# Expert layers: an expert's first unit is queued behind the next unit's transposes

## The chip, the core and the metric

The kernel runs on one core of one Trainium2 chip. That core has five engines that each take their own instructions in order: TensorE (PE in the profile; its weight loads, PEld, overlap its matmuls), VectorE (DVE), ScalarE (ACT), GpSimd (POOL) and SyncE (SP), which here only starts transfers. The metric is device microseconds of one execution, as the median of several timed runs. Besides the timed runs there is one execution taken by the hardware profiler, with a start and a duration for every instruction; "the span" is the time from its first to its last instruction. "The granted clock" is the share of full speed at which TensorE was allowed to run.

## The reference

The kernel computes four residual blocks on 8192 tokens of 256 features. Each block adds a normalised output to the running activations:

```
x = x + layernorm(attention_with_memory(layernorm(x)))
x = x + layernorm(mixture_of_experts_0(layernorm(x)))
x = x + layernorm(linear_attention(layernorm(x)))
x = x + layernorm(mixture_of_experts_1(layernorm(x)))
```

Only the two mixtures of experts matter here. Each has 8 experts. A gate sends every token to one expert; the tokens of an expert are ranked, and those beyond its capacity (512 in the first mixture, 1024 in the second) are dropped. An expert is two products with a nonlinearity between them:

```
h  = act(tokens_of_expert @ w1[e])      # 256 -> 1024, gelu in the first, relu in the second
eo = h @ w2[e]                          # 1024 -> 256
out = x + gate * eo[slot of the token]
```

All arithmetic is in float32. The output is (8, 1024, 256).

## The kernel before

The kernel goes through four stages: the attention with memory and its update (up to about 1292 us of the profiled span, the routing of the first mixture included), the first mixture's experts (about 1292 to 1602 us), the linear attention with the second routing (to about 2084 us), and the second mixture's experts (to the end, 2557.8 us). Both mixtures run through one function, `experts` (L954), called at L660 and L810. The routing has left, in DRAM, a row for every token and, on chip, the list of token numbers of every expert's slots and the number of tokens of every expert.

`experts` cuts each expert's slots into units of 256 slots (`UT`). The first mixture has two units per expert, 16 in all; the second has four, 32 in all. For a unit, these helpers do the work:

- `fetch(u)` (L974): two indirect transfers started by GpSimd (L814) gather 2 x 128 token rows into tile `d`. Five such tiles exist.
- `enter(d)` (L981): normalisation. VectorE takes the statistics (L144, L145: tiles `st_d`, `mv_d`, `ve_d`), GpSimd raises them to the power -1/2 (L133, tile `r_d`), VectorE writes the normalised rows `xh` with two instructions (`ln_apply`, L159) and scales `sc_d`.
- `turn(xh)` (L1004): four transposes on TensorE (L1009) into a PSUM tile `tp`, which VectorE copies to `dT` (one copy, L1011, in the second mixture; two instructions with scale and shift, L1014, in the first). Three `dT` and three `xh` tiles exist.
- `load(e)` (L1018): the two weight matrices `wa` and `wb` of an expert, started by SyncE, two sets of tiles.
- `products(u, ...)` (L1029): the unit's matmuls. The first product (L1037, tile `h`) is 16 matmuls in the code and 32 records in the profile, since a float32 matmul is two of them; ScalarE applies the nonlinearity (L1041 or L1045, `hT`); the second product (L1051, tile `op`) is 32 records. Then `finish0` (L635) or `finish1` (L786) add the residual and normalise on VectorE (L640 or L790 is its first instruction, per 128 rows), with a power on GpSimd (L133, `rs`), and the store goes out through SyncE (L658) or as a GpSimd scatter (L806).

The loop at L1064 goes over the units in order. In turn `u` it first starts the loads of the next expert, then `fetch(u+3)`, `enter(u+2)` and `turn(u+1)`, and then `products(u)`. An expert's first unit (`q == 0`) always runs and is not in a branch. Its later units stand in `tc.If(n[e] > q * UT)` (L1073): they are skipped on the chip where the expert has too few tokens. In the profiled execution 14 of 16 units ran in the first mixture and 20 of 32 in the second (1088 records of L1037, 32 for each unit).

The order of the instructions on each engine is not that of the code. A planner at build time lays them out: it follows the code's order as priority, but lets an instruction that it believes ready go ahead of an earlier one on the same engine that it believes is still waiting. A branch is one block for it: nothing from outside is mixed into it, though whole helpers can be put ahead of it or behind it. So parts of a first unit's `products`, which are outside any branch, may be placed among the `enter` and `turn` instructions of later units. On the chip each engine then follows its list strictly. `tc.issue_after(ins)` is the means to tell the planner more: every instruction that is traced inside it on the engine of `ins` must come behind `ins` in that engine's list. It adds no wait for `ins` to finish and no instruction.

Of the kernel before, what the change touches and what calls it, by code (L numbers as in the profile page):

```python
# [13 lines left out]
ALU = mybir.AluOpType  # L14
# [4 lines left out]
B, S, H = 8, 1024, 256  # L19
NTOK = B * S  # L20
P = 128
# [6 lines left out]
UT = TU * P  # L28
# [33 lines left out]
def sandwich_kernel(ctx: ExitStack, tc: tile.TileContext, a, out: bass.AP):  # L62
# [594 lines left out]
    def store0(s0, o):  # L657
        nc.sync.dma_start(_rows(slot0_d[s0 : s0 + UT, :]), o)  # L658

    experts(env, tok0_d, idx0[0], idx0[2], CAP0, a["wi"], a["wo"], AF.Gelu, None, None, finish0, store0, gbc)  # L660


# [150 lines left out]
def gather(nc, dst, src, idx):  # L813
    nc.gpsimd.indirect_dma_start(out=dst, out_offset=None, in_=src,  # L814
                                 in_offset=bass.IndirectOffsetOnAxis(ap=idx, axis=0),
                                 bounds_check=src.shape[0] - 1, oob_is_err=False)


class Router:
# [83 lines left out]
    def finish(self, pool):  # L903

        nc, nb = self.env.nc, self.nb
        tf = self.sb.tile([P, nb], F32, tag="tf", name="tf")
        nc.vector.tensor_scalar(tf, self.tab, -1.0, 0.0, ALU.add, ALU.max)
        got = pool.tile([P, nb], I32, name=f"got{nb}")
        nc.vector.tensor_copy(got, tf)
        tp = self.sb.tile([P, nb], F32, tag="tp", name="tp")  # L910
        nc.vector.tensor_scalar(tp, self.tab, 0.0, float(FAR), ALU.is_equal, ALU.mult)
        nc.vector.scalar_tensor_tensor(tp, self.tab, -1.0, tp, ALU.add, ALU.add)
        put = pool.tile([P, nb], I32, name=f"put{nb}")
        nc.vector.tensor_copy(put, tp)

        pc = self.ps.tile([P, NE], F32, tag="rt", name="pc")
        nc.tensor.matmul(pc, self.env.ones, self.before[:, :, TG], start=True, stop=True)
        cnt = pool.tile([P, NE], I32, name=f"cnt{nb}")
        nc.vector.tensor_copy(cnt, pc)
        return got, put, cnt  # L920
# [33 lines left out]
def experts(env, src, idx, cnt, cap, w1, w2, act, b1, b2, finish, store, gb):  # L954


    tc, nc, small = env.tc, env.nc, env.small
    with ExitStack() as ph:
        p2 = ph.enter_context(tc.tile_pool(name="e2", bufs=2))
        pc = ph.enter_context(tc.tile_pool(name="ec", bufs=1))  # L960
        p3 = ph.enter_context(tc.tile_pool(name="e3", bufs=3))
        p5 = ph.enter_context(tc.tile_pool(name="e5", bufs=5))
        pf = ph.enter_context(tc.tile_pool(name="ef", bufs=FC // 2 + 2))
        pst = ph.enter_context(tc.tile_pool(name="est", bufs=2, space=PSUM))
        psh = ph.enter_context(tc.tile_pool(name="esh", bufs=3, space=PSUM))
        pso = ph.enter_context(tc.tile_pool(name="eso", bufs=3, space=PSUM))
        if b1 is not None:
            b1c = pc.tile([P, NE * FC], F32, name="b1c")
            nc.sync.dma_start(b1c, b1)
        nq = cap // UT  # L970
        units = [(e, q) for e in range(NE) for q in range(nq)]
        nu = len(units)

        def fetch(u):  # L974
            d = p5.tile([P, TU, H + 1], F32, tag="d", name="d")
            for j in range(TU):
                i = u * TU + j
                gather(nc, d[:, j, :], src, idx[:, i : i + 1])
            return d

        def enter(d):  # L981

            mv = env.stats(env.tiles(d), "d")
            ve = small.tile([P, 2, TU], F32, tag="ve_d", name="ve_d")
            r = small.tile([P, 2, TU], F32, tag="r_d", name="r_d")
            nc.vector.tensor_scalar(ve[:, 0, :], mv[:, :, 1], EPS, None, ALU.add)
            if gb is None:
                env.rsqrt(r[:, 0, :], ve[:, 0, :], TU)
                rs = r[:, 0, :]
            else:  # L990
                nc.vector.tensor_scalar(ve[:, 1, :], mv[:, :, 1], 1.0 + EPS, EPS * EPS, ALU.mult, ALU.add)
                env.rsqrt(r.rearrange("p a t -> p (a t)"), ve.rearrange("p a t -> p (a t)"), 2 * TU)
                rs = r[:, 1, :]
            sc = p5.tile([P, 2, TU], F32, tag="sc_d", name="sc_d")
            s = d[:, :, H]
            if gb is not None:
                nc.vector.tensor_tensor(sc[:, 0, :], s, r[:, 0, :], ALU.mult)
            nc.vector.scalar_tensor_tensor(sc[:, 1, :], s, EPS, s, ALU.mult, ALU.mult)
            xh = p3.tile([P, TU, H], F32, tag="xh", name="xh")
            for j in range(TU):  # L1000
                env.ln_apply(xh[:, j, :], d[:, j, :H], mv, rs, j)
            return xh, sc

        def turn(xh):  # L1004
            dT = p3.tile([P, HC, UT], F32, tag="dT", name="dT")
            t = pst.tile([P, HC, UT], F32, tag="tp", name="tp")
            for c in range(HC):
                for j in range(TU):
                    nc.tensor.transpose(t[:, c, j * P : (j + 1) * P], xh[:, j, c * P : (c + 1) * P], env.ident)  # L1009
            if gb is None:  # L1010
                nc.vector.tensor_copy(dT, t)  # L1011
            else:
                for c in range(HC):
                    nc.vector.tensor_scalar(dT[:, c, :], t[:, c, :], gb[:, 0, c : c + 1], gb[:, 1, c : c + 1],  # L1014
                                            ALU.mult, ALU.add)
            return dT

        def load(e):  # L1018
            wa = p2.tile([P, HC, FF], F32, tag="wa", name="wa")
            nc.sync.dma_start(wa, w1[e].rearrange("(k p) f -> p k f", p=P))  # L1020
            wb = p2.tile([P, FC, H], F32, tag="wb", name="wb")
            nc.sync.dma_start(wb, w2[e].rearrange("(k p) f -> p k f", p=P))
            b2r = None
            if b2 is not None:
                b2r = p2.tile([P, H], F32, tag="b2r", name="b2r")
                nc.sync.dma_start(b2r, b2[e].partition_broadcast(P))
            return wa, wb, b2r

        def products(u, d, dT, sc, w):  # L1029
            e = units[u][0]  # L1030
            wa, wb, b2r = w
            hT = []
            for f0 in range(0, FC, 2):
                t = psh.tile([P, 2, UT], F32, tag="h", name="h")
                for f in range(2):
                    for c in range(HC):
                        nc.tensor.matmul(t[:, f, :], wa[:, c, (f0 + f) * P : (f0 + f + 1) * P], dT[:, c, :],  # L1037
                                         start=(c == 0), stop=(c == HC - 1))
                h = pf.tile([P, 2, UT], F32, tag="hT", name="hT")
                if b1 is None:  # L1040
                    nc.scalar.activation(h, t, act)  # L1041
                else:
                    for f in range(2):
                        i = e * FC + f0 + f
                        nc.scalar.activation(h[:, f, :], t[:, f, :], act, bias=b1c[:, i : i + 1])  # L1045
                hT.append(h)

            def po(j):
                t = pso.tile([P, H], F32, tag="o", name="op")
                for f in range(FC):  # L1050
                    nc.tensor.matmul(t, hT[f // 2][:, f % 2, j * P : (j + 1) * P], wb[:, f, :], start=(f == 0),  # L1051
                                     stop=(f == FC - 1))
                return t

            store(u * UT, finish(p2, d, po, b2r, sc))

        w = {0: load(0)}
        n = [nc.values_load(cnt[0:1, e : e + 1], min_val=0, max_val=NTOK,
                            skip_runtime_bounds_check_because="the experts' counts add up to NTOK")
             for e in range(NE)]  # L1060
        d = {u: fetch(u) for u in range(3)}
        x = {u: enter(d[u]) for u in range(2)}
        dT = {0: turn(x[0][0])}
        for u, (e, q) in enumerate(units):  # L1064
            if q == 0 and e + 1 < NE:
                w[e + 1] = load(e + 1)
            if u + 3 < nu:
                d[u + 3] = fetch(u + 3)
            if u + 2 < nu:
                x[u + 2] = enter(d[u + 2])  # L1070
            if u + 1 < nu:
                dT[u + 1] = turn(x[u + 1][0])
            with (tc.If(n[e] > q * UT) if q else nullcontext()):  # L1073
                products(u, d[u], dT[u], x[u][1], w[e])


# [41 lines left out]
```

## Time and profile before

| | |
|---|---|
| median of three timed runs | 2580.8 us (2579.83 to 2585.32) |
| the profiled execution's own time | 2559.46 us |
| its span | 2557.8 us |
| mean granted TensorE clock | 0.908 |
| TensorE busy | 2084.5 us, 81% |
| VectorE, ScalarE, GpSimd busy | 1156.3, 681.7, 749.7 us |
| first mixture's experts, 1292 to 1602 us | TensorE busy 227.32 of 310.00 us, granted clock 0.85 |
| second mixture's experts, 2084 to 2557.8 us | TensorE busy 314.88 of 473.80 us, granted clock 0.82 |

The profiled execution is 21.3 us shorter than the median of the timed runs, and a difference worked out in the trace is therefore added to the median, not compared with it. A row of the timeline has a start, a duration, the engine, the code line, the operation, the tile written and the tiles read, the shapes, how many instructions of the kind follow one another ("x32"), and in brackets the idle time of the engine before it with what ended that idle time. Consecutive rows of one engine show that engine's order, as the planner laid it out. A row of the windows gives the window, its length, the busy time of the engine with its number of instructions, the granted clock, and the transfers' share and rate.

### The profile page before, as it was taken

To read this page: it belongs to the slowest core of one execution; us is meant where nothing else is said; L and a number is where in the kernel's file an instruction comes from. 1 tells how busy PE (TensorE), PEld (TensorE's weight loads), DVE (VectorE), ACT (ScalarE), POOL (GpSimd) and SP (SyncE) were. 2 spreads that over 40 slices of the span, in tenths; PEclk is the share of its full clock that TensorE was granted. 3 is DMA by queue.
4 is the path that set the end of the run, shared out by engine and by line. 5 is a ranking of instruction groups with operands and counts; after the bars stand their busy time and mean duration, and the time that the engine had idled before them with its cause. 6 is when DMAs were issued, how large, how long until landed. Compare 5 with 4: busy or idle time off the path is not lost. (4 is left out here: it accounts for less than half of the span.)

```text
span 2557.8 us, 25355 instructions
## 1 busy us (share of the span) xinstructions
PE 2084.5 (81%) x8441; PEld 1442.0 (56%) x8441; DVE 1156.3 (45%) x4272; ACT 681.7 (27%) x1187; POOL 749.7 (29%) x811
## 2 busy tenths in 40 slices
PE   5999999998999899889758778689898846885387
PEld 4556555555565556556547566346555545664276
DVE  4445453356455645564533333046565643333232
ACT  3554554232323232322101111223332201111021
POOL 2121220134343433343441221741111123333322
PEclk8999999899999999999869889799999958887698
DMA  4110100201010001000051320111111141122300
GB/s 137 45 50 34 50 25 32 96 25 33 25 40 27 34 25 41 25 25 17 17 157 54 95 91 9 52 33 42 42 42 42 50 116 61 60 68 70 94 23 16
DMA packets 89010, 129.31 MB, mean 51 GB/s; under 512 B 8403, under 2 KB 74104, under 8 KB 88740
## 3 DMA queue, kind: packets, MB, share of 16 engines
q1 hardware_dynamic: 74612, 98.23, 11.6%
q0 software_dynamic: 10640, 24.32, 3.7%
q10 hardware_dynamic: 3616, 4.99, 0.6%
q8 instruction: 74, 1.21, 0.2%
q14 instruction: 68, 0.56, 0.1%
HBM read 86.99 MB, written 46.82 MB: 52 GB/s over the span
## 5 line engine op out<-in xcount | busy, mean ns | idle before, releaser
L1037 PE MATMUL h<-dT,wa 128*128 128x256 f32 x1088 | 271.4, 411 | 4.1 <-issue 2.4
L182 PE MATMUL mm<-x2T,w_W1T 128*128 128x512 f32 x512 | 249.9, 630 | 0.0
L1037 PEld LDWEIGHTS h<-dT,wa 128*128 128x128 f32 x1088 | 225.3, 210 | 43.4 <-issue 7.9
L1051 PE MATMUL op<-wb,hT 128*128 128x256 f32 x1088 | 240.4, 379 | 0.0
L550 PE MATMUL ff<-w_W2T,fT 128*128 128x256 f32 x1024 | 231.1, 381 | 0.0
L1051 PEld LDWEIGHTS op<-wb,hT 128*128 128x128 f32 x1088 | 206.7, 190 | 28.1
L1009 PE MATMUL tp<-ident,xh 128*128 128x128 f32 x192 | 39.8, 359 | 219.8 <-DVE xh L159 219.8
L550 PEld LDWEIGHTS ff<-w_W2T,fT 128*128 128x128 f32 x1024 | 191.1, 190 | 24.5 <-issue 0.5
L1045 ACT ACTIVATE hT<-h,b1c 128x256 f32<-128x256 f32 x160 | 67.1, 470 | 399.0 <-PE h L1037 399.0
L1009 PEld LDWEIGHTS tp<-ident,xh 128*128 128x128 f32 x192 | 28.5, 174 | 230.8 <-issue 140.9
L182 PEld LDWEIGHTS mm<-x2T,w_W1T 128*128 128x128 f32 x512 | 98.9, 204 | 98.8 <-issue 98.1
L545 ACT ACTIVATE fT<-mm,cols 128x512 f32<-128x512 f32 x128 | 88.0, 687 | 199.8 <-PE mm L182 199.7
L594 POOL TENSOR_TENSOR e<-euler,d 128x32 f32<-128x32 f32 x16 | 87.0, 5439 | 179.8 <-DVE d L845 179.8
L702 PE MATMUL kv<-w_WqkvT,xnT 128*128 128x512 f32 x256 | 123.0, 614 | 5.0 <-ACT xnT L690 4.9
L814 POOL DMA_INDIRECT d<-tok_d,got x96 | 100.0, 1042 | 75.3 <-DMA wb<-in_w_dram 16.5
L695 PE MATMUL pm<-kv 128*128 128x257 f32 x256 | 73.2, 411 | 44.2 <-ACT kv L707 38.0
L133 POOL TENSOR_TENSOR rs<-ve,mhalf 128x2 f32<-128x2 f32 x34 | 24.0, 707 | 289.4 <-DVE ve L644 191.6
L695 PEld LDWEIGHTS pm<-kv 128*128 128x128 f32 x256 | 46.8, 197 | 92.7 <-issue 66.3
L1041 ACT ACTIVATE hT<-h 128x512 f32<-128x512 f32 x56 | 33.3, 597 | 239.7 <-PE h L1037 239.7
L507 ACT ACTIVATE moT<-mm,bmo 128x512 f32<-128x512 f32 x32 | 22.0, 687 | 263.0 <-PE mm L182 263.0
L790 DVE TENSOR_TENSOR o<-op,b2r 128x256 f32<-128x256 f32 x40 | 16.9, 423 | 151.7 <-PE op L1051 150.6
L843 DVE TENSOR_REDUCE mx<-lg 128x4 f32<-128x32 f32 x32 | 6.1, 191 | 173.8 <-PE lg L840 173.8
(308 smaller groups left out, 4067.5 us busy)
## 6 DMA issues: line engine op xcount, KB each, us to landing
tok_d<-xa SPq DMA_DIRECT2D x16, 514.0 KB, 3.4
tok_d<-xf SPq DMA_DIRECT2D x16, 514.0 KB, 3.5
xg<-in_x_dram SPq DMA_DIRECT2D x16, 512.0 KB, 3.9
x1T_d<-x1T SPq DMA_DIRECT2D x16, 512.0 KB, 3.3
x1T<-x1T_d SPq DMA_DIRECT2D x16, 512.0 KB, 3.3
xa<-in_x_dram SPq DMA_DIRECT2D x16, 512.0 KB, 3.9
wa<-in_wi_dram SPq DMA_DIRECT2D x8, 1024.0 KB, 6.6
wb<-in_wo_dram SPq DMA_DIRECT2D x8, 1024.0 KB, 9.1
```

The lines of the kernel that those rows point to most:

```text
L182: mm = nc.tensor.matmul(t, w[:, k, o * P : (o + 1) * P], v, start=(k == 0), stop=(k == len(k_in) - 1))
L545: lambda o, t: nc.scalar.activation(fT[o], t, AF.Silu, bias=col("b1", o)))
L550: mm = nc.tensor.matmul(t, fT[f][:, j * P : (j + 1) * P], w2_[:, f, :], start=(f == 0), stop=(f == FC - 1))
L594: nc.gpsimd.tensor_tensor(e, env.euler, d, ALU.pow)
L695: mm = nc.tensor.matmul(pm[d], kvs[j][:, d * P : (d + 1) * P], kvs[j][:, H:], start=(first and j == 0), stop=(last and j == TG - 1))
L702: nc.tensor.matmul(t, xnT[:, c, j * P : (j + 1) * P], wqkv[:, c, H:], start=(c == 0), stop=(c == HC - 1))
L814: nc.gpsimd.indirect_dma_start(out=dst, out_offset=None, in_=src, in_offset=bass.IndirectOffsetOnAxis(ap=idx, axis=0), bounds_check=src.sh ...
L1009: nc.tensor.transpose(t[:, c, j * P : (j + 1) * P], xh[:, j, c * P : (c + 1) * P], env.ident)
L1037: nc.tensor.matmul(t[:, f, :], wa[:, c, (f0 + f) * P : (f0 + f + 1) * P], dT[:, c, :], start=(c == 0), stop=(c == HC - 1))
L1041: nc.scalar.activation(h, t, act)
L1045: nc.scalar.activation(h[:, f, :], t[:, f, :], act, bias=b1c[:, i : i + 1])
L1051: nc.tensor.matmul(t, hT[f // 2][:, f % 2, j * P : (j + 1) * P], wb[:, f, :], start=(f == 0), stop=(f == FC - 1))
```

## The change

`enter` and `turn` now also return instructions: `enter` the last `xh` instruction, `turn` the last transpose and the last copy to `dT`. In the loop, the products of a first unit are traced inside `tc.issue_after` for three instructions: the last `xh` instruction of unit `u+2` (VectorE), the last transpose of unit `u+1` (TensorE) and the last copy to `dT` of unit `u+1` (VectorE). So every TensorE instruction of these products comes behind that transpose in TensorE's list, and every VectorE instruction of them behind the other two in VectorE's. The instructions of the products on ScalarE, GpSimd and SyncE get no such order. Units in branches are as they were. No instruction is added or taken away.

```
-                env.ln_apply(xh[:, j, :], d[:, j, :H], mv, rs, j)
-            return xh, sc
+                last = env.ln_apply(xh[:, j, :], d[:, j, :H], mv, rs, j)
+            return xh, sc, last
...
-                    nc.tensor.transpose(t[:, c, j * P : (j + 1) * P], xh[:, j, c * P : (c + 1) * P], env.ident)
+                    tr = nc.tensor.transpose(t[:, c, j * P : (j + 1) * P], xh[:, j, c * P : (c + 1) * P], env.ident)
             if gb is None:
-                nc.vector.tensor_copy(dT, t)
+                ev = nc.vector.tensor_copy(dT, t)
             else:
                 for c in range(HC):
...
+                    ev = nc.vector.tensor_scalar(dT[:, c, :], t[:, c, :], gb[:, 0, c : c + 1], gb[:, 1, c : c + 1],
+                                                 ALU.mult, ALU.add)
-            return dT
+            return dT, tr, ev
...
-        dT = {0: turn(x[0][0])}
+        dT = {0: turn(x[0][0])[0]}
         for u, (e, q) in enumerate(units):
...
             if u + 2 < nu:
                 x[u + 2] = enter(d[u + 2])
+            first = []
+            if u + 2 < nu:
+                first.append(x[u + 2][2])
             if u + 1 < nu:
-                dT[u + 1] = turn(x[u + 1][0])
-            with (tc.If(n[e] > q * UT) if q else nullcontext()):
+                dT[u + 1], *did = turn(x[u + 1][0])
+                first += did
+            with ExitStack() as order:
+                if q:
+                    order.enter_context(tc.If(n[e] > q * UT))
+                else:
+                    for ins in first:
+                        order.enter_context(tc.issue_after(ins.ins))
                 products(u, d[u], dT[u], x[u][1], w[e])
```

## The prediction

> **What bounds the kernel now.** I read the page first, then the table of waits for the two expert stages, then TensorE's timeline through both, then VectorE's and GpSimd's around a few first units, and last the granted clock. The page's costliest groups and the waits of the two stages (engine, line, releaser, total, times, longest):
>
> ```profile
> L1009 PE MATMUL tp<-ident,xh 128*128 128x128 f32 x192 | 39.8, 359 | 219.8 <-DVE xh L159 219.8
> ...
> PE tp L1009 <- DVE xh L159: 71.4, 9, 9.7
> ...
> PE tp L1009 <- DVE xh L159: 148.4, 9, 25.1
> ```
>
> In both stages TensorE's idle time is one kind of wait: the transposes of a unit wait for its normalised rows. 71.4 of the 219.8 us lie in the first mixture, 148.4 in the second. Its other gaps there come to a few us, so the stage's length is TensorE's work plus these waits. TensorE's order in the first mixture, around expert 2, and the start of expert 1 in the second:
>
> ```profile
> 1353.04 7.07 PE L1037 MATMUL h<-dT,wa 128*128 128x256 f32 x32
> 1359.95 7.07 PE L1051 MATMUL op<-wb,hT 128*128 128x256 f32 x32
> 1366.86 1.03 PE L1037 MATMUL h<-dT,wa 128*128 128x256 f32 x4
> 1377.08 1.22 PE L1009 MATMUL tp<-ident,xh 128*128 128x128 f32 x4 [9.19 <-DVE xh L159]
> 1378.09 8.58 PE L1037 MATMUL h<-dT,wa 128*128 128x256 f32 x28
> 1386.51 7.07 PE L1051 MATMUL op<-wb,hT 128*128 128x256 f32 x32
> 1393.42 0.60 PE L1009 MATMUL tp<-ident,xh 128*128 128x128 f32 x4
> ...
> 2140.76 1.99 PE L1009 MATMUL tp<-ident,xh 128*128 128x128 f32 x8 [21.11 <-DVE xh L159]
> 2143.09 9.31 PE L1037 MATMUL h<-dT,wa 128*128 128x256 f32 x32 [0.34 <-issue]
> ```
>
> Unit 4 is expert 2's first. Four of its 32 h-matmuls stand ahead of unit 5's transposes and fill 0.9 us of the wait; 28 stand behind. In the second mixture all 32 stand behind. What the transposes of unit 5 wait for is a chain through GpSimd and VectorE:
>
> ```profile
> 1372.32 1.09 POOL L814 DMA_INDIRECT d<-tok_d,got  x1 [0.25 <-DVE mv_d L145]
> 1373.44 0.74 POOL L133 TENSOR_TENSOR o<-ve,mhalf 128x2 f32<-128x2 f32 x1
> 1374.36 1.06 POOL L814 DMA_INDIRECT d<-tok_d,got  x1 [0.18 <-issue]
> 1375.45 1.05 POOL L133 TENSOR_TENSOR r_d<-ve_d,mhalf 128x4 f32<-128x4 f32 x1
> ...
> 1371.87 0.16 DVE L991 TENSOR_SCALAR ve_d<-mv_d 128x2 f32<-128x2 f32 x1
> ...
> 1376.61 0.73 DVE L159 TENSOR_SCALAR xh<-d,mv_d,r_d 128x256 f32<-128x256 f32 x2
> ...
> 1379.62 0.99 DVE L1014 TENSOR_SCALAR dT<-tp,gbc 128x256 f32<-128x256 f32 x2
> 1390.17 0.48 DVE L640 SCALAR_TENSOR_TENSOR o<-d,sc_d,op 128x256 f32<-128x256 f32 x1 [9.55 <-PE op L1051]
> ```
>
> Nothing in it reads what the four matmuls write.
>
> **The change part by part.** It adds and removes no instruction; it can only reorder lists. There are 16 first units, eight per mixture, and three orders for each.
>
> VectorE's two orders: the products' first instruction (L640 or L790) behind the next unit's dT and the second next unit's xh. In the rows above dT ends at 1380.61 and L640 starts at 1390.17 after an idle 9.55 us that the second product ended; the xh of unit 6 (0.73 us at 1378.90) also stands ahead. I looked at the other first units of both stages the same way: dT and xh stand ahead in all, with 6.8 us of idle time or more before L640 or L790. These orders move nothing. Were that cover gone, the held instruction would cost two xh and a dT, 0.73 + 0.99 = 1.72 us a unit.
>
> TensorE's order in the second mixture: in all eight experts 32 h-matmuls follow directly on the transposes, as at 2140.76. Nothing moves. The same holds for expert 0 of the first mixture. So 9 of the 16 first units are already as asked.
>
> TensorE's order in experts 1 to 7 of the first mixture: h x4 stands ahead of the wait in six of them (starting 1325.40, 1366.86, 1407.67, 1448.55, 1476.82, 1517.66) and h x2 in expert 7 (1555.07). 6 x 4 + 2 = 26 matmuls leave the wait and go behind the transposes. Their price is the warm one: x32 from 1353.04 to 1359.95 is 6.91 us, 0.216 us each; the slow stretch after the wait keeps its place, and the matmuls that are more come at the end of the run. 26 x 0.216 = 5.6 us, 0.86 us for each of six experts and 0.43 for the last. All of it is on the path: from 1377.08 to the next wait TensorE has no idle time, and the next wait's chain starts from the last second product (L640, then the powers, the gather, r_d, xh), so a run that ends later by 0.86 us moves that chain by the same. The wait itself starts earlier and ends when it did: 9.19 becomes 10.05 us.
>
> The other queues. ScalarE's first activation of the unit needs eight h-matmuls and comes 4 x 0.42 us later; it takes 0.60 us for every 1.73 us of h-matmuls, so the second product still follows on directly; if not, 0.60 us per expert. SyncE's stores and weight loads and GpSimd's powers, gathers and scatters get no order: they follow VectorE's results and the release of tiles, and those move with TensorE. The weights of the next expert are asked for tens of us ahead (6.6 and 9.1 us to land by the page).
>
> What the trace can't show is whether the planner, given the new orders, lays out other instructions differently. I bound it by GpSimd's rows. Five of the seven waits (experts 1 to 5) have gathers just ahead of r_d; the last two have none, and are shorter (6.40 and 6.80 us). One more gather ahead of r_d would cost 1.06 us and its 0.30 us of issue, 1.36 us x 5 = 6.8 us. With r_d where the first gather stands, right behind its input (ve_d ends at 1372.03), 1375.45 - 1372.32 = 3.13 us x 5 = 15.7 us would be gained. I take zero, because what stands around there hangs on the products' own tail, which shifts as a whole.
>
> The clock. Where the wait ended, TensorE ran at half speed for a stretch:
>
> ```profile
> 1377.08:1382.89 5.81, 5.81 (x16) 0.50 0.98 318
> 1382.89:1386.00 3.11, 3.11 (x16) 1.00 0.11 39
> 1417.88:1423.85 5.97, 5.97 (x16) 0.50 0.94 338
> 1423.85:1427.00 3.15, 3.15 (x16) 1.00 0.02 7
> ```
>
> The seven stretches are 5.53, 5.81, 5.97, 5.73, 4.32, 4.58 and 4.75 us. They end at 1341.93, 1382.89, 1423.85, 1464.81, 1492.12, 1529.66 and 1567.21: distances of 40.96, 40.96, 40.96, 27.31, 37.54 and 37.55 us, or 12, 12, 12, 8, 11 and 11 steps of 3.413 us. So the end sits on a grid, and a start that is late by d within one step gets d/2 back, while one that passes into the next step pays 1.71 us more. By that, the delay at the starts of units 4, 6, 8, 10 is 0.86, 1.29, 1.51, 1.62; unit 10 has only 4.32 - 3.41 = 0.91 us to spare and pays, and the delay after units 10, 12 and 14 is 3.4, 4.3 and 4.3 us. In the second mixture seven more waits pull it towards one or two whole steps, 3.4 or 6.8 us. Where the grid lies in the timed runs no row shows (they spread over 5.5 us, 1.6 steps), so I keep 3.4 and 6.8 as ends and take the matmuls' own 5.6, which lies between.
>
> The Trainium skill, "TensorE: Matmul & The Clock Gate", Part 1 (What's actually happening), says that the activity window of 3413 ns runs freely and that one should not fit to a count of slow matmuls. The rows agree with the 3.41 us; by the rule the sum stays at 5.6, by this trace's grid it would be 4.3. The same page ("Why this matters for your kernels") advises against idle gaps over about 3 us between bursts, which speaks against taking work out of such a gap; here both the gap of 9.2 us and one of 10.05 are past it.
>
> The sum: 2559.46 + 5.6 = 2565.1 us for the profiled execution. The median stands 21.3 us above that execution, a difference that I carry: 2580.8 + 5.6 = 2586.4 us, 0.22% more. A measurement of this kernel can tell about 0.2%, 5.2 us, from no change.
>
> **The rivals.**
>
> Later r_d. The planner's new order puts one more gather ahead of r_d in the first mixture. For it: GpSimd's list already has gathers there, and gathers that are thought ready go in early. Against: they wait for tiles that the branch releases. 5.6 + 6.8 = 12.4: 2593.2 us.
>
> Earlier r_d, the case on the other side. With the h-matmuls held, the planner's clock of a first unit is later, and r_d of the next unit takes the place of the gather at 1372.32. For it: its input is ready 3.4 us before it starts. Against: in the five waits r_d stands behind the last gather each time, and GpSimd gets no order from the change. It saves 3.13 us a wait: 5.6 - 15.7 = -10.1, 2570.7 us; it decides from 5.6 / 5 = 1.1 us a wait on.
>
> It changes nothing that counts: the new orders are met as they are, or the clock's grid takes the delay in: 0 to 3.4 us, 2580.8 to 2584.2. For it: 9 of 16 units are met already. Against: seven times h stands ahead of the transposes.
>
> **How the numbers follow.** The forecast, 26 matmuls moved and little else: 0.68, with 2583 to 2590 as its own range (one grid step to two, and the median's own scatter). Its middle lies just past the 0.2% bound, so I count 0.46 of it as slower and 0.22 as within. Later r_d 0.13, slower. Nothing that counts 0.04, within. Earlier r_d 0.15, faster. Slower 0.59, within 0.26, faster 0.15. The range reaches to both r_d cases and past the later one by the scatter: 2571 to 2596.
>
> **What would show it.** In the changed profile TensorE's list of the first mixture should show no h between a second product and a wait for xh, and h x32 behind each tp; the waits of the first stage some 0.9 us longer each (71.4 to about 77); the second stage's list as before; r_d in its place on GpSimd, and the slow stretches shorter where a start moved within its step. The forecast is wrong if GpSimd's list around r_d differs, if the second stage's lists differ, or if unit 4's transposes start more than a few us from 1377.

## The result, and the profile after

The changed kernel takes 2584.04 us (median of 20 runs, 2573.24 to 2590.82), against 2580.86 us for the kernel before in the same set (20 runs, 2571.42 to 2585.32): a ratio of 1.001, with a 95% interval of 1.0 to 1.0021, or +2.6 us (0 to +5.4). That is within the 0.2% that was called the limit of the measurement. The two medians differ by 3.2 us. The forecast of 2586.4 us was 2.4 us too long, and its +5.6 us lies just above the interval. The profiled execution took 2579.56 us, its span 2577.9 us, with a granted clock of 0.908.

The transposes' group on the page of the changed kernel, then its waits in the two expert stages:

```profile
L1009 PE MATMUL tp<-ident,xh 128*128 128x128 f32 x192 | 39.9, 358 | 227.4 <-DVE xh L159 227.3
```

```profile
PE tp L1009 <- DVE xh L159: 79.7, 9, 11.8
...
PE tp L1009 <- DVE xh L159: 147.6, 9, 24.5
```

The wait for the normalised rows has grown by 8.3 us in the first mixture (71.4 before) and not in the second (148.4 before). TensorE's order around expert 2, and the start of expert 1 in the second mixture, in the timeline of the changed kernel:

```profile
1356.61 7.07 PE L1051 MATMUL op<-wb,hT 128*128 128x256 f32 x32
1373.74 1.23 PE L1009 MATMUL tp<-ident,xh 128*128 128x128 f32 x4 [10.06 <-DVE xh L159]
1374.76 9.00 PE L1037 MATMUL h<-dT,wa 128*128 128x256 f32 x32
1383.59 7.07 PE L1051 MATMUL op<-wb,hT 128*128 128x256 f32 x32
...
2164.29 1.99 PE L1009 MATMUL tp<-ident,xh 128*128 128x128 f32 x8 [20.93 <-DVE xh L159]
```

No h stands between the second product and the wait; all 32 stand behind the transposes. The wait is 10.06 us (9.19 before), and the second mixture's order is the old one. GpSimd and VectorE around the same place, in the timeline of the changed kernel:

```profile
1371.02 1.06 POOL L814 DMA_INDIRECT d<-tok_d,got  x1 [0.18 <-issue]
1372.11 1.05 POOL L133 TENSOR_TENSOR r_d<-ve_d,mhalf 128x4 f32<-128x4 f32 x1
...
1387.25 0.48 DVE L640 SCALAR_TENSOR_TENSOR o<-d,sc_d,op 128x256 f32<-128x256 f32 x1 [9.98 <-PE op L1051]
```

r_d still stands behind its two gathers, and L640 still waits some 10 us for the second product. Over the whole program the lists of ScalarE, GpSimd and SyncE are those of before. VectorE's differs in one thing: in six units one instruction of 0.15 us (L998, a scale for a later unit) has changed places with the copies to dT. TensorE's differs in the 26 records that were foretold.

**Where the time went.** From the first transpose of the first mixture's experts to the end of their last second product, in the windows of the kernel before and of the changed one (window, length, busy time and count of TensorE, its weight loads, VectorE, ScalarE and GpSimd, granted clock, transfers):

```profile
1305.19:1592.69 287.50, 223.57 (x960) 190.20 (x960) 97.63 (x378) 34.61 (x57) 59.62 (x82) 0.87 0.25 76
```

```profile
1301.12:1592.71 291.59, 221.23 (x960) 189.41 (x960) 97.67 (x378) 34.61 (x57) 59.66 (x82) 0.87 0.25 75
```

The stage is 4.1 us longer. TensorE's idle time in it grew by 6.4 us (63.93 to 70.36), and the same 960 matmuls took 2.3 us less (223.57 to 221.23). The second number is the clock. The waits of experts 1, 5 and 6 before and after show how it works:

```profile
1325.40 1.28 PE L1037 MATMUL h<-dT,wa 128*128 128x256 f32 x4 [0.84 <-DVE dT L1014]
1336.40 1.22 PE L1009 MATMUL tp<-ident,xh 128*128 128x128 f32 x4 [9.72 <-DVE xh L159]
...
1487.80 1.22 PE L1009 MATMUL tp<-ident,xh 128*128 128x128 f32 x4 [9.70 <-DVE xh L159]
...
1525.08 1.22 PE L1009 MATMUL tp<-ident,xh 128*128 128x128 f32 x4 [6.40 <-DVE xh L159]
```

```profile
1332.23 1.22 PE L1009 MATMUL tp<-ident,xh 128*128 128x128 f32 x4 [11.84 <-DVE xh L159]
...
1485.19 1.22 PE L1009 MATMUL tp<-ident,xh 128*128 128x128 f32 x4 [11.81 <-DVE xh L159]
...
1524.21 1.22 PE L1009 MATMUL tp<-ident,xh 128*128 128x128 f32 x4 [7.27 <-DVE xh L159]
```

Set on expert 1's wait (1336.40 against 1332.23, a shift of 4.17 us), the delay is 1.56 us at expert 5's (1487.80 - 1485.19 = 2.61, and 4.17 - 2.61) and 3.30 us at expert 6's (0.87 by the same working). Without the clock it would have been four times 0.86 us and five times 0.86 us: 3.4 and 4.3. The half-speed tails behind the waits for unit 5 and unit 11 in the changed kernel:

```profile
1373.74:1378.63 4.89, 4.89 (x14) 0.50 1.03 348
1378.63:1382.00 3.37, 3.37 (x17) 1.00 0.32 111
1485.19:1491.28 6.09, 6.09 (x16) 0.50 0.58 179
1491.28:1494.50 3.22, 3.22 (x16) 1.00 0.00 0
```

Unit 5's tail shrank from 5.81 to 4.89 us, since its end stayed on the grid while its start came later. Unit 11's grew from 4.32 to 6.09 us, since its start had passed into the next step of 3.413 us. Both were foretold. The seven tails of the changed kernel end at 1337.69, 1378.65, 1419.61, 1460.57, 1491.29, 1528.84 and 1566.38 us, which is 12, 12, 12, 9, 11 and 11 steps of 3.413 us from one to the next; before it was 12, 12, 12, 8, 11 and 11. That one step, 3.4 us, is most of the 4.1.

**What is not the change.** The profiled span is 20.1 us longer, but 24 us of difference lie in the linear attention, whose lists are the same: from the start of the first mixture's last second product to the second mixture's first transpose it took 512.97 us before and 537.15 us after. Two of TensorE's waits in its first 130 us in the changed kernel's profile do not occur in that of the kernel before:

```profile
PE kv L702 <- issue: 13.7, 2, 9.4
...
PE pm L695 <- issue: 11.1, 3, 7.9
```

"issue" is a wait for nothing that the profile shows. More on it stands below, with the carried 21.3 us.

### The profile page after: what moved, and what is told of

Its sections match the earlier page's. It is cut to its first block, busy times and chain, and to the rows that moved or that the text cites. A ratio compares the mean times of both kernels' runs of the same rounds, so it can differ in the third digit from the quotient of the medians.

```text
span 2577.9 us, 25348 instructions
## 1 busy us (share of the span) xinstructions
PE 2074.5 (80%) x8441; PEld 1434.4 (56%) x8441; DVE 1156.7 (45%) x4272; ACT 681.9 (26%) x1187; POOL 750.1 (29%) x811
## 5 line engine op out<-in xcount | busy, mean ns | idle before, releaser
L1037 PE MATMUL h<-dT,wa 128*128 128x256 f32 x1088 | 265.6, 406 | 2.4 <-issue 2.4
L1051 PEld LDWEIGHTS op<-wb,hT 128*128 128x128 f32 x1088 | 206.7, 190 | 28.1
L550 PEld LDWEIGHTS ff<-w_W2T,fT 128*128 128x128 f32 x1024 | 191.1, 190 | 24.5 <-issue 0.5
L702 PE MATMUL kv<-w_WqkvT,xnT 128*128 128x512 f32 x256 | 128.5, 637 | 25.3 <-issue 13.7
L814 POOL DMA_INDIRECT d<-tok_d,got x96 | 100.1, 1043 | 76.3 <-DMA wb<-in_w_dram 17.4
L702 PEld LDWEIGHTS kv<-w_WqkvT,xnT 128*128 128x128 f32 x256 | 50.3, 206 | 74.2 <-issue 51.0
```

What stands on the lines that cost most here:

```text
L550: mm = nc.tensor.matmul(t, fT[f][:, j * P : (j + 1) * P], w2_[:, f, :], start=(f == 0), stop=(f == FC - 1))
L702: nc.tensor.matmul(t, xnT[:, c, j * P : (j + 1) * P], wqkv[:, c, H:], start=(c == 0), stop=(c == HC - 1))
```

## The experiments

All times are compared with runs of the kernel before in the same set. "The stage" is the stretch of the two windows above, to the start of the last second product: 280.43 us before, 284.52 us changed. The kernels with a number "ahead" put that many matmul records of an expert's first unit in front of the next unit's transposes, in the first mixture alone; the kernel before has 4 there (2 in expert 7, all 32 behind in expert 0), the changed one none. Where the expectation with 16 ahead says "calls", read 16 records, which are 8 calls, and 4 records in the kernel before; in that with 48 ahead read 32 and 16 records. The sums there are in records.

### Each order by itself

```
# vector orders only            # tensor order only
-    first += did               -    first += did
+    first += did[1:]           +    first = did[:1]
```

> Only the two orders on VectorE (products of a first unit behind the xh of the second next and the dT of the next unit), not the one on TensorE. By the prediction these two are met already, so every engine's list, the four matmuls ahead of each wait included, stays as before: time 1.000 of before, within 0.1%, and from the first transpose of the first mixture to the start of its last second product about 280.4 us as before (after: 284.5). If the two orders cost something, the 1.72 us a unit of the prediction's cover would show as 7 x 1.72 = 12 us. A second purpose: the profiled execution of before took 2559.5 us, less than all its timed runs (2571 to 2585). If that one execution was unusual, this profile has a linear attention stage some 20 us longer than the 493 us of that one; if 2559.5 is usual under the profiler, it is 493 again.

Measured: 2553.21 against 2553.6 us, ratio 1.000 (0.999 to 1.0009). The stage is 280.37 us, and all five lists are those of the kernel before.

> Only the order on TensorE (products of a first unit behind the next unit's last transpose). If that is all the change does, lists and time are those of the changed kernel: +3 us (0.12%), with 284.5 us from the first transpose of the first mixture to the start of its last second product. Price of the 26 matmuls alone, with the slow stretches of the clock unchanged: 280.4 + 5.6 = 286.0 us. By the clock's grid of 3.41 us: 284.7 us wherever the grid lies. Rival, the 3 us of the changed kernel are scatter of the linear attention stage: then the time is 1.000 of before and that stage takes what it does in the run with the VectorE orders alone.

Measured: 2557.57 us, ratio 1.0011 (1.0001 to 1.0021), or +2.8 us. The stage is 284.88 us, and all five lists are those of the changed kernel, the moved L998 included. So TensorE's one order is the whole change, and the others ask for what is there already. The grid repeats too: the tails again end 12, 12, 12, 9, 11 and 11 steps apart, and the same one, that of unit 11, is a step longer.

### How much of the wait is filled

The first unit's products call back after a given number of records, and trace the next unit's transposes there, behind the matmul just issued and ahead of the rest:

```
+                if ahead == 4 * (f0 + 2):
+                    turn_now(mm)
...
+                if ahead == 48 and j == 0:
+                    turn_now(mm)
```

The first place is inside the first product, the second between the halves of the second product. In all these kernels the lists of ScalarE and GpSimd are those of the kernel before. VectorE's differs in where the two copies to `dT` of expert 0's second unit stand, and with 48 ahead also in that the first half's residual (L640) stands ahead of copies to `dT`.

> First mixture only: 8 records of a first unit's first product stand ahead of the next unit's transposes (before: 4, after: 0). Nothing else moves but TensorE's list. Price of the matmuls alone: 4 x 0.216 x 6 and 6 x 0.216 = 6.5 us less than before. With the clock's grid: 5.5 us less, and single slow stretches between 3.4 and 6.8 us. If filling the wait were worth nothing (its end moves with its start), 0.

Measured: 2547.9 us, ratio 0.9971 (0.9959 to 0.9982). The stage is 275.29 us, 5.1 less than before. The idle time fell by 5.3 us and not by the price's 6.5, because expert 0, where 8 records now stand ahead too, lost 1.1 us: its first product waits 2.87 us for a copy, where TensorE waited 1.76 us for the second transposes before. The busy time stayed as it was.

> First mixture only: all 32 records of a first unit's first product stand ahead of the next unit's transposes, the reverse of the change. The matmuls' price alone, slow stretches as before: 28 x 0.216 x 6 + 30 x 0.216 = 42.8 us less than before in the first mixture. If the wait left over (10.2 - 6.9 = 3.3 us, under one grid step of 3.41) no longer lets the clock drop, the slow stretches go as well: about 60 us less, 2520 us. Rival: the next wait's chain was hidden by the old length of the run, the wait comes back elsewhere and less than 30 us are gained.

Measured: 2505.1 us, ratio 0.980 (0.9779 to 0.982). The stage is 230.92 us, 49.5 less, between the two theories' numbers: five waits of 3.1 to 3.7 us are left, and each still has one step of half speed; two are down to 0.3 us and have none.

> In the first mixture the first unit of an expert issues 16 of its first product's matmul calls (32 records) ahead of the next unit's transposes, where the kernel before issues 6 x 2 calls in experts 1 to 7. Theory that each record that leaves the wait costs its warm price, 0.216 us, and each that fills it gives that back: from the run with 8 calls ahead (-5.7 us against the kernel before) a further 7 x 8 records x 0.216 = 12.1 us, so -18 us. Theory that the half-speed stretches hang on a free-running grid of 3.413 us, so that a shorter wait also takes a step of the slow stretch away in some of the units: -21 to -24 us. If the waits were filled by something else than TensorE's order, within 3 us of the run with 8 ahead.

Measured: 2556.82 us against 2579.92, ratio 0.9907 (0.9891 to 0.9924), which is -24.0 us (-19.6 to -28.1). The stage is 260.30 us, 20.1 less. The price alone, -18, is outside the interval of the time; the grid's -21 to -24 is inside it. The stage's 20.1 us lies between the two: 17.4 us less idle time, which is the price, and 2.7 us at a better clock.

> In the first mixture the next unit's transposes stand between the two halves of the first unit's second product: all the 32 calls of the first product and the first 8 of the second one are ahead of them. The wait for the normalised rows is then to vanish in all seven experts (in the run with 32 ahead, 3.1 to 3.7 us of it were left in five of them). Price alone, from that run's -48.5 us: it can give back no more than the waits that were left, 26.9 us, so between -48 and -75 us; with the half-speed stretches gone as well, -79 us. A rival: the wait does not go, it changes its place (VectorE's copies of the transposes are then late for the next unit's first product, as 2.5 us in expert 0 with 32 ahead): then no better than -52 us.

Measured: 2502.41 us, ratio 0.9692 (0.9671 to 0.9714), 3.1% faster than the kernel before, and the best of all that were run. The stage is 204.81 us, 75.6 less. Waits of the stage, its timeline around unit 5, and the windows over the stage, in the kernel with 48 ahead:

```profile
PE tp L1009 <- DVE xh L159: 8.9, 3, 8.4
```

```profile
1366.32 0.74 PE L1009 MATMUL tp<-ident,xh 128*128 128x128 f32 x4
1366.90 3.62 PE L1060 MATMUL op<-wb,hT 128*128 128x256 f32 x16
1370.35 0.60 PE L1009 MATMUL tp<-ident,xh 128*128 128x128 f32 x4
1370.79 7.07 PE L1044 MATMUL h<-dT,wa 128*128 128x256 f32 x32
```

```profile
1303.64:1515.52 211.88, 206.87 (x960) 178.32 (x960) 96.15 (x378) 34.73 (x57) 60.02 (x83) 0.98 0.34 104
```

The transposes at 1366.32 have no bracket: the wait is gone, and so is every half-speed stretch but the one at the stage's start (granted clock 0.98). Of the 75.6 us, 58.9 are idle time (63.93 to 5.01), and 16.7 are the same 960 matmuls at a better clock (223.57 to 206.87). The price alone does not reach that far: the 26.9 us of waits in the expectation hold 9.1 us ahead of the stage's first transposes, which this order can't fill, so it ends at -48.5 - 17.8 = -66 us. The rival, that the wait moves to VectorE's copies, is 2.9 us in expert 0; in all the waits for copies come to 4.5 us, against 1.7 before.

| records ahead | stage, us | TensorE idle, us | TensorE busy, us | against before: idle, busy |
|---|---|---|---|---|
| 0 (the change) | 284.52 | 70.36 | 221.23 | +6.4, -2.3 |
| 4 (before) | 280.43 | 63.93 | 223.57 | |
| 8 | 275.29 | 58.59 | 223.77 | -5.3, +0.2 |
| 16 | 260.30 | 46.51 | 220.86 | -17.4, -2.7 |
| 32 | 230.92 | 21.99 | 216.00 | -41.9, -7.6 |
| 48 | 204.81 | 5.01 | 206.87 | -58.9, -16.7 |

The idle and busy times are taken to the end of the last second product, 7.07 us further. From 8 to 32 ahead the idle time falls by 0.216 to 0.219 us a record (12.1 us for 7 x 8 records, 24.5 for 7 x 16): the warm price. The busy time does not follow the records; the runs with useless matmuls below show that it goes by the clock.

### The same order in the second mixture too

```
-            if q == 0 and gb is not None:
+            if q == 0 and u + 1 < nu:
```

> As the run with 48 ahead, and the same order in the second mixture, whose waits at the first units are for other things (the kernel before has its second mixture's products already behind the transposes' neighbours in the order that the changed kernel asks for). Theory that the first mixture's gain is all that the order can give: within 5 us of the run with 48 ahead in the first mixture alone. If the second mixture's first units also stand in a wait for the normalised rows that filling takes away: some 20 to 60 us below it. If the later transposes delay the second units there: above it.

Measured: 2517.31 us, ratio 0.9761 (0.9741 to 0.9781), 14.9 us more than with 48 ahead in the first mixture alone. The first mixture is the same (204.56 us); from the second's first transpose to the end it takes 469.4 us, against 457.3. Waits there, with 48 ahead in the first mixture and in both:

```profile
PE tp L1009 <- DVE xh L159: 147.2, 9, 24.4
PE h L1044 <- issue: 2.4, 7, 0.3
```

```profile
PE tp L1009 <- DVE xh L159: 145.9, 8, 24.4
PE h L1044 <- issue: 8.4, 7, 1.2
PE h L1044 <- DVE dT L1011: 3.6, 1, 3.6
```

TensorE's order at expert 1 of the second mixture, with 48 ahead in both:

```profile
2084.69 1.14 PE L1009 MATMUL tp<-ident,xh 128*128 128x128 f32 x4 [21.11 <-DVE xh L159]
2087.02 9.63 PE L1044 MATMUL h<-dT,wa 128*128 128x256 f32 x32 [1.20 <-issue]
```

The order fills nothing there: the long wait is for normalised rows too, but it is that of the first unit's own transposes, which stand ahead of its products, so none of them can go into it. It adds 6.0 us of "issue" and one wait of 3.6 us for a copy, and the waits for the normalised rows behind the first transposes are 2.0 us shorter (127.8 against 129.8). The same 1408 records take 318.60 us in place of 314.27, at a mean granted clock of 0.82 in place of 0.83: 4.3 us more. Together that is 11.9 of the 12.1 us.

### The clock by itself

With 8 records ahead, useless matmuls are put in the wait, so that no real work changes its place:

```
+                old, wa, m = fill
+                for k in range(m):
+                    nc.tensor.matmul(t[:, k % HC, :], wa[:, 0, :P], old[:, 0, :], start=True, stop=True)
...
+                    fill = (dT[u], w[e][0], 17 if e < 6 else 10) if e else None
```

The half-filled kernel has 8 and 5 in place of 17 and 10. Apart from the useless records, the lists of TensorE, VectorE, ScalarE and GpSimd are those of the kernel with 8 ahead.

> The order of the run with 8 records ahead (275.3 us from the first transpose of the first mixture's experts to the start of the last second product, -5.7 us against the kernel before), and in experts 1 to 7 useless matmuls between those records and the transposes: 17 calls, that is 34 records or 7.3 us, where that run waits 8.3 to 8.9 us, and 10 calls, 4.3 us, where it waits 5.5 us. They write the tile that the transposes then overwrite. No work leaves the wait or joins it, so the idle time is merely used up. Theory that the half-speed stretches after the waits are the clock's answer to idle time: they ran 34 us in that run (3.4, 5.5, 3.3, 5.2, 4.9, 5.7 and 6.3 us behind the transposes), half of which is lost, so that the stage becomes about 17 us shorter and the time -20 to -24 us against the kernel before. Theory that what counts is only which matmuls lie in the wait: as the run with 8 ahead, -4 to -8 us.

Measured: 2533.79 us against 2559.78, ratio 0.9901 (0.9884 to 0.9917), or -25.3 us (-21.2 to -29.7). The stage is 259.20 us, 16.1 less than with 8 ahead unfilled. Timeline and windows of the filled kernel around unit 5's transposes:

```profile
1363.78 1.89 PE L1048 MATMUL h<-dT,wa 128*128 128x256 f32 x8
1365.51 7.50 PE L1010 MATMUL tp<-dT,wa 128*128 128x256 f32 x34
1374.01 0.87 PE L1013 MATMUL tp<-ident,xh 128*128 128x128 f32 x4 [1.00 <-DVE xh L159]
1374.71 5.35 PE L1048 MATMUL h<-dT,wa 128*128 128x256 f32 x24
```

```profile
1374.01:1378.01 4.00, 4.00 (x20) 1.00 1.00 329
```

The 34 useless records end in time, 1.00 us of idle is left, and the 24 h behind run at full speed. Over the stage the busy time without the useless records is 253.34 - 46.47 = 206.87 us, or 208.0 us if what overlaps with them is counted as real work; with 48 ahead it was 206.87 us, with 8 ahead unfilled 223.77. So the 16.7 us of busy time are the clock's, and the clock answers to idle time, whether the matmuls that fill it are useful or not.

> As the run before it, with 8 calls (3.5 us) in the long waits and 5 calls (2.2 us) in the two short ones, so that about 4.9 and 3.3 us of idle time are left. If the loss goes by the steps of 3.413 us that the idle time touches: one step of half speed is left after most waits, and the stage is 6 to 12 us shorter than with 8 ahead unfilled (the run with 32 ahead, with 3.1 to 3.7 us idle, had TensorE busy 7.8 us less than the one with 8 ahead). If idle time up to about 5 us costs nothing: as the filled run, 17 us shorter. If any idle time costs the same: no shorter than with 8 ahead.

Measured: 2552.07 us, ratio 0.9973 (0.9964 to 0.9983). The stage is 275.73 us, no shorter than unfilled: the third case. The half-speed tail does not go by the length of the wait. Around unit 7's transposes, unfilled (timeline and window) and half-filled (timeline and windows):

```profile
1416.42 1.22 PE L1009 MATMUL tp<-ident,xh 128*128 128x128 f32 x4 [8.32 <-DVE xh L159]
```

```profile
1416.42:1419.70 3.28, 3.28 (x10) 0.50 1.03 381
```

```profile
1407.30 3.62 PE L1010 MATMUL tp<-dT,wa 128*128 128x256 f32 x16
1415.78 1.23 PE L1013 MATMUL tp<-ident,xh 128*128 128x128 f32 x4 [4.87 <-DVE xh L159]
```

```profile
1415.78:1419.10 3.32, 3.32 (x10) 0.50 1.02 386
1419.10:1422.00 2.90, 2.90 (x15) 0.99 0.78 275
```

Half the idle time was gone, yet the tail behind the wait is 3.3 us as before. A shorter wait takes half-speed time away inside the wait, where it costs nothing. The tail is set by where on the grid the wait ends. It is what is left of that step and, unless that step was busy almost from its start, one step more: 3.2 to 6.2 us behind the waits of experts 1 to 7 in all these runs, where the clock had dropped before the wait's end. Here the wait ended about 0.1 us into a step, and no further slow step came. With 32 ahead the slow step began within 1 us of the wait's end, and it was the only one. Around unit 7's transposes, windows of the kernel with 32 ahead:

```profile
1405.51:1409.80 4.29, 4.29 (x13) 0.61 1.04 382
1409.80:1413.00 3.20, 3.20 (x16) 0.99 0.27 96
```

## Why the prediction was right

**VectorE's orders move nothing.** Right: alone they give the lists of before and a ratio of 1.000. One scale of 0.15 us (L998) changes places with dT in the changed kernel, but with TensorE's order alone it does so too, so it comes with that order; no wait of TensorE in the stage is for it.

**Nine of 16 first units are as asked.** Right: all of the second mixture and expert 0 are unchanged in TensorE's list.

**26 matmuls leave the wait at 0.216 us, 5.6 us on the path.** The mechanism and the price were right. The idle time grew by 6.4 us: 26 x 0.216 = 5.6 us, and 0.84 us because the four h of experts 1 and 5 had run at 1.28 us for four, not at 0.86, behind a wait of 0.84 us for dT (the row at 1325.40). Those two experts also explain the waits: 79.7 us and not about 77, since twice 0.84 us of idle time that had stood under dT now stands under xh, and twice 0.42 us of slow h is idle instead.

**The other queues, the two r_d rivals.** Zero was right: GpSimd's list is that of before, and r_d stands where it stood. Both rivals are out: nothing came ahead of r_d, and it did not move forward.

**The clock.** Here a term of the sum was mis-sized. The prediction worked out 0.86, 1.29, 1.51 and 1.62 us of delay, then 3.4, 4.3 and 4.3, and then took 5.6, the matmuls' own price, as lying between two grid steps. The waits of the profile, set on expert 1's, give 0.83, 1.25, 1.46 and 1.56, then 3.30 and 4.18, and the stage +4.1 us (+4.5 with TensorE's order alone). The grid's number was the better one, and it was in the text. The idle time's 0.84 us beyond the price is paid by slow matmuls that are gone; the clock gives back the other 1.5 us of the 2.3.

This term also carried the chances to the wrong side. With 4.3 us the forecast would have been 2585.1 us, 0.17% more; with 5.6 us it stood just past 0.2%, and 0.59 went to a time that is measurably slower, which +2.6 us is not. The time alone even leaves no change open (0 to +5.4 us), and the stated range, 2571 to 2596 us, is wide enough to hold both r_d cases, so it is the lists and the stage that bear the mechanism out, and not that the time lies in the range.

The Trainium skill, "TensorE: Matmul & The Clock Gate", Part 1 (What's actually happening), advises against fitting to a count of slow matmuls, since the window runs freely. For one ramp at a kernel's start no run here tells; for waits that follow one another the two executions with this order show about the same end of the chain, +4.1 and +4.5 us, since each slow tail ends on the grid (the whole steps above) and so sets where in its step the next wait ends.

**The second mixture's pull to 3.4 or 6.8 us.** Not settled. From its first transpose to the end it took 459.2 us before and 456.5 with the same lists in another execution, and 455.1 and 455.5 us with the change: 1.0 to 4.1 us less, where two executions with the same lists differ by 2.7.

**The carried 21.3 us.** The profile of before stood 21.3 us below its median, and carrying that was right, for a reason the prediction did not have. In the sets where the kernel before took 2553.6 and 2559.78 us, the six profiles of experiments have 509 to 513 us from the start of the first mixture's last second product to the second mixture's first transpose; the three of the set where it took 2579.92 us, on the same chip as the first of these, and the changed kernel's profile have 532 to 537 us. That goes with the set and not with the kernel, and the profile of before (512.97 us) belongs to the shorter kind.

**"Nothing that counts".** This rival's bracket (2580.8 to 2584.2 us) holds the measured time, as the forecast's own range (2583 to 2590) does. The time alone can't tell them apart; the stages can, with 284.5 and 284.9 us against 280.4 in two executions each: 4.1 us or more in the stage, where the rival allowed 3.4 at most.

## What to carry to other kernels

Price a reordering by what it takes out of a wait or puts into it, record by record at the warm rate, and look up in the lists which places already have the order that is asked for. Where the wait also costs the clock, add that as a second term, and work it in steps from where the wait ends: halving the long waits brought none of it, cutting them to 3.1 to 3.7 us (two of seven to 0.3) brought 7.6 us, and removing them brought 16.7 us. A long wait in front of an engine's list is an invitation to look for work that is ready and stands behind it: 48 records ahead of the transposes gave 3.1%, where the change took the last four away for 0.1%.

## What the runs showed of the hardware

The tail of half speed does not grow with the wait. With 8 ahead, unfilled and half-filled, waits of 3.35 to 8.9 us had tails of 3.3 to 6.2 us, and the stage was the same with long and with half-filled waits (275.29 and 275.73 us); the filled kernel's waits of 0.99 to 1.53 us had none. So less than a whole step of idle time is enough to lose the clock: the wait of 3.14 us (1402.37 to 1405.51) was followed by a slow step that the clock's record begins at 1406.43, and in the 3.41 us before that TensorE had been idle for 2.5 and busy for 0.9.

What decides is the idle time within one step of the grid. Over the first mixture's stage in all eleven profiles, a step at full speed with 2.13 us or more of idle time was followed by half speed, and one with 2.00 us or less was not. A step at half speed with 0.44 us or less of idle time was followed by full speed, and one with 0.62 us or more by another at half speed. The steps nearest the first bound, in the kernel before and with 8 ahead, each with the step behind it (window, length, busy time and count of TensorE, granted clock, transfers):

```profile
1324.87:1328.28 3.41, 1.28 (x4) 1.00 0.73 238
1328.28:1331.70 3.42, 0.00 (x0) 0.50 0.43 137
```

```profile
1327.56:1330.97 3.41, 1.42 (x6) 1.00 0.71 290
1330.97:1334.38 3.41, 0.00 (x0) 1.00 0.30 77
```

The Trainium skill, "TensorE: Matmul & The Clock Gate", Part 1 (What's actually happening), gives an idle window of about 3.4 us as what it takes to fall to half clock. By these rows 2.13 us of idle time within one window is enough, and 2.00 us is not; the bound lies between.

One kernel on one chip took 2553.6 us in one set and 2579.92 us in another, with spreads of 13 and 5 us. Where profiles of such sets differ, it is in about the first 110 us of the linear attention: TensorE waits longer there, in part for "issue" (24.8 us in the changed kernel's profile) and in part for ScalarE, which itself waits 19.3 us for what the profile calls "remote". What these waits are for, no run here shows.
